# A graph layer's set-up reordered: the table of places turned, gather indices and raw rows' statistics moved

## The chip, the cores and the metric

The kernel runs on one core of a Trainium2 chip. The metric is the device time of one execution in microseconds (us), as the median over several executions; less is better. Below, PE is the matrix engine, PEld its weight loads, DVE the vector engine, ACT the scalar engine, POOL the GpSimd engine and SP the queue that issues most DMA transfers.

## What is computed

`x` holds 12,500 nodes with 128 features; 200,000 edges go from `src` to `dst` and are sorted by `dst`. The reference, cut down:

```python
h = jnp.maximum(_layernorm(x), 0.0)
Qv, Ku = h @ W_Q.T, h @ W_K.T
score = einsum('md,md->m', Qv[dst], Ku[src]) / sqrt(128) * exp(-edge_weight)
# of each dst node's edges keep the 16 of highest score; softmax over those
alpha = w / denom[dst]
agg = segment_sum(alpha[:, None] * (h[src] @ W_msg.T), dst)
out = x + relu(h @ W_self.T + agg)
```

## The kernel before

**Work units.** The edges are cut into 112 groups (`G`) of 14 chunks (`GC`) of 128 edges. For each chunk one indirect DMA, issued by POOL (`gather`, line 176), fetches 128 rows of 512 bytes into one of eight rotating tiles `hs`. A group takes 14 of them, so there are 1563 gathers in all (56 from `x`, 1507 from `h_tab`; the last group is short). POOL does hardly anything else.

**Raw groups.** Groups 0 to 3 (`RAW = 4`) are gathered from `x` itself, before the normalized table exists, and are normalized after the gather. All later groups are gathered from `h_tab`, a table of `relu(layernorm(x))` that the set-up writes to DRAM. Gathers from `h_tab` are let go two at a time by `let_go` (line 183): DVE copies two columns of indices into a small tile `ix`, and POOL waits for that copy. A gather of group g + 8 also waits until the last reader of group g's `hs` tile is done, which is the second half of `sums` (line 674) three passes after the group's own pass.

**Set-up (lines 278 to 421).** SP loads the source indices `src_r`, then `x` in six pieces, then weights, `dst_r` and `ew_r`, in that order. DVE clears tables, casts the indices (line 335), takes the statistics of `x`'s first piece (line 336), and copies the indices, turned by PE, to `idx_all` (line 338), which lets POOL begin. `row_stats` is one `bn_stats` for each row block (line 200), six small DVE operations and a square root on ACT (line 212). `normed` is a reciprocal and a product on DVE (lines 217 and 218) and one Relu activation on ACT for each row block (line 220). After `x`'s last piece, DVE makes from `dst_r` the tables `rel` (line 381), `h0` (384) and its running count `h1` (scan, line 386). PE turns them and DVE (line 397) and ACT (lines 400 and 401) write them to `pd`, a bfloat16 table of 128 x 112 x 2 x 16. For one edge of a chunk `pd` holds its place in its node's list and its node's distance in the group. ACT then writes the decay factors (line 402).

**Passes.** The main loop runs passes i from -3 to 117. It is a software pipeline: pass i makes the one-hot tables of group i + 1 (`edges_turned`, `far_of`, `away`, `to_edges`, `places`), the scores of group i, sorts scores into slots of group i - 1, picks the best 16 of group i - 2, and forms the weighted sums of group i - 3. The schedule is by hand: each engine executes its instructions strictly in the order of the program text, so an instruction that waits holds up all behind it on its engine.

On ACT a pass goes: the turned places `pdT` (line 550), four `far` squares (536), first `aw` square (559), two more `aw`, `to_e` (541), `hT` (517), `opo` (563). The `far` and `aw` matrices share one PSUM bank (`"a"`) with each other and with `sums`, so PE and ACT alternate there. In passes -1 to 2, `raw_stats(i + 1)` stands at the start of the pass, ahead of `pdT` on ACT through its square root, and `raw_normed(i + 1)` stands between the first and second `aw`.

`later` (line 440) is a list of checks on `pd` and others, one DVE operation in each pass from pass 1 on. DVE's `best` (line 613) and `scores` (line 583) and the copies of `let_go` fill the rest.

Of the kernel before, what the change touches and what calls it, by code (L numbers as in the profile page):

```python
# [10 lines left out]
F32 = mybir.dt.float32  # L11
BF16 = mybir.dt.bfloat16
# [8 lines left out]
P = 128  # L21
# [35 lines left out]
def lead(j):  # L57
    return STEP * j - PRE
# [7 lines left out]
def upper(ap):  # L66

    return ap.bitcast(BF16).rearrange("p (n two) -> p n two", two=2)[:, :, 1]
# [8 lines left out]
def gnn_layer(  # L77
# [35 lines left out]
    assert G > TAIL  # L113
# [41 lines left out]
    pd = const.tile([P, G, 2, 16], BF16, name="pd")  # L155
    dlw = pd[:, :, 1, 0:NJ]
# [23 lines left out]
    def gather_at_once(g, table):  # L180
        gather(g, 0, own[g], lambda j: idx_all[:, GC * g + j:GC * g + j + 1], table)

    def let_go(g, k):

        j0, j1 = 2 * k, min(2 * k + 2, own[g])
        if j0 >= j1:
            return
        if k == 0:
            T[g]["ix"] = rows_pool.tile([P, GC], I32, name="ix", bufs=7)
        ix = T[g]["ix"]  # L190
        nc.vector.tensor_copy(ix[:, j0:j1], idx_all[:, GC * g + j0:GC * g + j1])  # L191
        gather(g, j0, j1, lambda j: ix[:, j:j + 1])

    def row_stats(pool, rows, n, name, between=lambda: None):

        st = pool.tile([rows.shape[0], n, 6], F32, bufs=1, name=f"st{name}")
        for t in range(n):
            if t == 3:
                between()
            nc.vector.bn_stats(st[:, t, :], rows[:, t, :])  # L200
# [10 lines left out]
        nc.vector.tensor_scalar(rs, rs, 1.0 / D, EPS, op0=OP.mult, op1=OP.add)  # L211
        nc.scalar.sqrt(rs, rs)
        return rs, sm

    def normed(rows, n, rs, sm):

        nc.vector.reciprocal(rs, rs)
        nc.vector.scalar_tensor_tensor(sm, sm, -0.5, rs, op0=OP.mult, op1=OP.mult)
        for t in range(n):
            nc.scalar.activation(rows[:, t, :], rows[:, t, :], AF.Relu, bias=sm[:, t:t + 1],  # L220
                                 scale=rs[:, t:t + 1])

# [17 lines left out]
    with tc.tile_pool(name="edges", bufs=1) as ep, ExitStack() as stage:  # L240
# [48 lines left out]
        make_identity(nc, ident)  # L289
        nc.gpsimd.iota(dst_r, pattern=[[1, RL + P]], base=1 << 21, channel_multiplier=0)  # L290
# [3 lines left out]
        for p0, p1 in sixteens(1, k):  # L294
# [4 lines left out]
        nc.gpsimd.iota(slots, pattern=[[1, KM]], base=0, channel_multiplier=0,  # L299
                       allow_small_or_imprecise_dtypes=True)  # L300
        nc.gpsimd.iota(nvec, pattern=[[0, 1]], base=0, channel_multiplier=1,
                       allow_small_or_imprecise_dtypes=True)

        jj, eq = (alz[0][0:32, NJ * KM * k:NJ * KM * (k + 1)].rearrange("p (j k) -> p j k", k=KM) for k in range(2))
        nc.gpsimd.iota(jj, pattern=[[1, NJ], [0, KM]], base=0, channel_multiplier=0,
                       allow_small_or_imprecise_dtypes=True)
# [9 lines left out]
        nc.vector.memset(pd, 1.0)  # L316
        nc.vector.memset(dec_all[:, RR * CPR:CW], 0.0)
        nc.vector.tensor_scalar(minus, nvec, -1.0, None, op0=OP.mult)
        for j in range(NJ):
            nc.vector.memset(w0[:, j:j + 1], float(lead(j)))  # L320
# [8 lines left out]
        nc.vector.memset(alz[0], 0.0)  # L329
        for k in range(2):  # L330
            nc.vector.memset(sl1[k][:, :, KM:], 1.0)


        src_f = src_r.bitcast(F32)[:, 0:RW]
        nc.vector.tensor_copy(src_f, src_r[:, 0:RW])
        stat = {0: row_stats(prep, xs[0][2], sizes[0], "x0")}
        by_chunk = lambda t: t[:, 0:RR * CPR].rearrange("e (p j) -> e j p", j=CPR)
        to_columns(src_f, 0, lambda at, p: nc.vector.tensor_copy(at(by_chunk(idx_all)), p))
        for g in range(min(RAW, G)):
            gather_at_once(g, x)  # L340

        def finish(i):
            t0, n, xg = xs[i]
            normed(xg, n, *stat[i])
# [37 lines left out]
        let_go(RAW, 2)  # L382
        nc.vector.memset(h0[:, 0:1], 0.0)
# [3 lines left out]
        let_go(RAW, 4)  # L387
        bb = rows_pool.tile([P, 2, G], F32, name="bb")
        nc.vector.tensor_copy(bb, pb[:, 0:2 * G].rearrange("p (a g) -> p a g", a=2))

        for j0 in range(0, NJ, 4):
            j1 = min(j0 + 4, NJ)
            pt = bank("q", 3)
            for j in range(j0, j1):
                nc.tensor.matmul(pt[:, (j - j0) * RR:(j - j0 + 1) * RR], lhsT=rel[:, j * P:(j + 1) * P],
                                 rhs=upper(ident[0:RR, 0:RR]), start=True, stop=True)
            nc.vector.tensor_tensor(dlw.rearrange("e g j -> e j g")[:, j0:j1, :],
                                    pt[:, 0:(j1 - j0) * RR].rearrange("e (j g) -> e j g", g=RR),
                                    bc(w0[:, j0:j1], RR), op=OP.subtract)
        to_columns(h1, HALO, lambda at, p: nc.scalar.copy(at(pd[:, :, 0, :].rearrange("e g j -> e j g")), p))  # L400
        nc.scalar.copy(pd[:, 0:G - 1, 0, GC:NJ], pd[:, 1:G, 0, 0:1])
# [30 lines left out]
    def all_checked():  # L432
# [15 lines left out]
        lambda: nc.vector.tensor_reduce(badc[:, 0:1], pd[:, :, 0, 0:NJ], axis=AX.XY, op=OP.max),  # L448
# [32 lines left out]
    with tc.tile_pool(name="win", bufs=2) as win:  # L481
# [23 lines left out]
        def raw_stats(g):  # L505
            T[g]["raw"] = row_stats(rows_pool, T[g]["hs"], own[g], "r")

        def raw_normed(g):
            normed(T[g]["hs"], own[g], *T[g]["raw"])


# [195 lines left out]
        def at(g, stage, *args):  # L707
            if 0 <= g < G:
                stage(g, *args)


        for i in range(-3, G + 6):
# [5 lines left out]
            if i + 1 < RAW:  # L718
                at(i + 1, raw_stats)

# [29 lines left out]
            if i + 1 < RAW:  # L750
                at(i + 1, raw_normed)
# [28 lines left out]
            at(i, scores_in_slots)  # L780
            more(6)
# [187 lines left out]
```

## Time and profile before

| what | value |
|---|---|
| median of 4 runs | 2058.99 us (2058.85 to 2059.57) |
| the profiled execution | 2056.74 us |
| its span, first to last instruction | 2054.9 us |
| what lies around the span | 1.84 us |
| busy in the span | PE 81%, POOL 74%, DVE 62%, ACT 51% |
| mean granted PE clock | 0.896 |
| first gather begins | 15.75 us |
| last gather begins | 2010.53 us |

The profile is of one execution. "Busy" counts time inside instructions; a gather counts 0.94 us and is followed by at least 0.30 us in which POOL issues it, so POOL can be full at 74%. A line of the timeline is: start in us, length in us, engine, line of the kernel, operation, output<-inputs, and in brackets how long the engine was idle before and what ended that. A line of the waits is: total us, number of times, longest.

### The profile page before, as it was taken

To read this page: it belongs to the slowest core of one execution; us is meant where nothing else is said; L and a number is where in the kernel's file an instruction comes from. 1 tells how busy PE (TensorE), PEld (TensorE's weight loads), DVE (VectorE), ACT (ScalarE), POOL (GpSimd) and SP (SyncE) were. 2 spreads that over 40 slices of the span, in tenths; PEclk is the share of its full clock that TensorE was granted. 3 is DMA by queue.
4 is the path that set the end of the run, shared out by engine and by line. 5 is a ranking of instruction groups with operands and counts; after the bars stand their busy time and mean duration, and the time that the engine had idled before them with its cause. 6 is when DMAs were issued, how large, how long until landed. Compare 5 with 4: busy or idle time off the path is not lost. (4 is left out here: it accounts for less than half of the span.)

```text
span 2054.9 us, 42100 instructions
## 1 busy us (share of the span) xinstructions
PE 1658.2 (81%) x13800; PEld 1327.1 (65%) x13801; DVE 1272.3 (62%) x6998; ACT 1044.5 (51%) x2198; POOL 1511.0 (74%) x1580
## 2 busy tenths in 40 slices
PE   0367899999888898888888888889888888888895
PEld 0246777777666676666667676667676666666674
DVE  7547767676666656565656665666566556666653
ACT  6756555555444454444544444555455444445440
POOL 5775777777777777777777777777777777777772
PEclk9958999999998989898988988998889898989987
DMA  9511222222222222222222222222222222222210
GB/s 228 168 57 46 74 68 66 68 65 69 65 64 63 65 65 65 65 64 65 65 66 64 65 62 63 65 65 65 65 64 65 65 65 65 65 61 66 65 57 18
DMA packets 101472, 143.46 MB, mean 70 GB/s; under 512 B 31063, under 2 KB 74327, under 8 KB 100480
## 3 DMA queue, kind: packets, MB, share of 16 engines
q0 software_dynamic: 50144, 102.74, 17.6%
q1 hardware_dynamic: 51102, 37.99, 6.7%
q8 instruction: 108, 1.77, 0.4%
q14 instruction: 118, 0.97, 0.2%
HBM read 126.79 MB, written 14.40 MB: 69 GB/s over the span
## 5 line engine op out<-in xcount | busy, mean ns | idle before, releaser
L176 POOL DMA_INDIRECT hs<-h_tab,ix x1507 | 1442.4, 957 | 475.1 <-issue 278.9
L583 DVE SCALAR_TENSOR_TENSOR prod<-hs,dec_all,q 128x128 f32<-128x128 f32 x1674 | 499.4, 345 | 184.2 <-DMA hs<-h_tab,ix 144.9
L574 PEld LDWEIGHTS q<-q,to_e 128*128 128x128 f32 x3348 | 482.0, 217 | 73.6 <-issue 59.7
L574 PE MATMUL q<-q,to_e 128*128 128x128 f32 x3348 | 525.8, 306 | 0.0
L536 ACT ACTIVATE far<-a,minus 128x512 bf16<-128x512 f32 (+1 forms) x447 | 295.2, 660 | 374.5 <-PE a L534 365.7
L674 PE MATMUL a<-hs,alz 128*128 128x128 f32 x3348 | 450.2, 290 | 11.1 <-ACT aw L559 0.4
L674 PEld LDWEIGHTS a<-hs,alz 128*128 128x128 f32 x3348 | 420.0, 203 | 22.0 <-ACT aw L559 18.5
L613 DVE TENSOR_SCALAR ell<-slots,e 128x40 f32<-128x40 f32 x112 | 28.7, 256 | 472.6 <-PE e L599 469.1
L599 PEld LDWEIGHTS e<-opo,sl 128*41 128x41 f32 x3348 | 178.6, 134 | 101.3 <-issue 90.0
L534 PE MATMUL a<-rel,ident 112*128 112x512 bf16 (+1 forms) x447 | 192.2, 430 | 43.8 <-ACT far L536 26.9
L559 ACT ACTIVATE aw<-a 128x400 bf16<-128x400 f32 x336 | 168.6, 502 | 110.3 <-PE a L557 110.3
L599 PE MATMUL e<-opo,sl 128*41 128x40 f32 x3348 | 219.4, 224 | 0.0
L541 ACT ACTIVATE to_e<-far 128x1920 f32<-128x1920 bf16 x112 | 200.5, 1790 | 0.0
L557 PE MATMUL a<-minus_at,pdT 32*128 32x400 bf16 x336 | 119.7, 356 | 92.6 <-ACT aw L559 76.6
L682 PE MATMUL s<-ident,agn 128*128 128x128 f32 x112 | 40.2, 359 | 155.1 <-DVE o L694 150.5
L679 ACT ACTIVATE agn<-a,rden 128x128 f32<-128x128 f32 x112 | 41.2, 368 | 206.7 <-PE a L674 206.7
L583 DVE DVE_READ_ACCUMULATOR prod<-hs,dec_all,q 128x1 f32 x1674 | 140.7, 84 | 0.0
L563 ACT ACTIVATE opo<-aw 128x1200 f32<-128x1200 bf16 x112 | 136.1, 1215 | 0.0
L191 DVE COPY ix<-idx_all 128x2 int32<-128x2 int32 x754 | 128.7, 184 | 0.0
L682 PEld LDWEIGHTS s<-ident,agn 128*128 128x128 f32 x112 | 16.5, 148 | 168.4 <-DVE o L694 160.6
L642 PEld LDWEIGHTS <-to_e 128*128 128x128 bf16 x1674 | 52.1, 99 | 98.6 <-DVE prod L583 85.4
L550 ACT CAST pdT<-a 32x128 bf16<-32x128 f32 x112 | 28.5, 254 | 162.1 <-PE a L547 162.1
(172 smaller groups left out, 1737.3 us busy)
## 6 DMA issues: line engine op xcount, KB each, us to landing
hs<-h_tab,ix POOLq DMA_INDIRECT x1507
h_r<-h_tab SPq DMA_DIRECT2D x112, 64.0 KB
x_t<-in_x_dram SPq DMA_DIRECT2D x108, 64.0 KB
out_dram<-o SPq DMA_DIRECT2D x108, 64.0 KB
xg<-in_x_dram SPq DMA_DIRECT2D x2, 1400.0 KB
h_tab<-xg SPq DMA_DIRECT2D x2, 1400.0 KB
xg<-in_x_dram SPq DMA_DIRECT2D x1, 1120.0 KB
h_tab<-xg SPq DMA_DIRECT2D x1, 1120.0 KB
```

Source lines behind the costliest of these rows:

```text
L176: nc.gpsimd.indirect_dma_start(out=T[g]["hs"][:, j, :], out_offset=None, in_=table[0:N, :], in_offset=bass.IndirectOffsetOnAxis(ap=index(j ...
L191: nc.vector.tensor_copy(ix[:, j0:j1], idx_all[:, GC * g + j0:GC * g + j1])
L534: nc.tensor.matmul(pr[:, 0:n1 - n0], lhsT=upper(ident[0:RR, g:g + 1]).to_broadcast([RR, P]), rhs=rel[:, n0:n1], start=True, stop=True)
L536: nc.scalar.activation(T[g]["far"][:, n0:n1], pr[:, 0:n1 - n0], AF.Square, bias=minus)
L541: nc.scalar.activation(T[g]["to_e"][:, 0:n], T[g]["far"][:, 0:n], AF.Relu, bias=1.0, scale=-1.0)
L557: nc.tensor.matmul(pr[:, 0:400], lhsT=T[g]["pdT"], rhs=minus_at.rearrange("k w j s -> k (w j s)")[:, n0:n1], start=True, stop=True)
L559: nc.scalar.activation(T[g]["aw"][:, n0:n1], pr[:, 0:400], AF.Square)
L563: nc.scalar.activation(T[g]["opo"].rearrange("e w j s -> e (w j s)"), T[g]["aw"], AF.Relu, bias=1.0, scale=-1.0)
L574: nc.tensor.matmul(pq[:, (j - j0) * P:(j - j0 + 1) * P], lhsT=T[g]["to_e"][:, j * P:(j + 1) * P], rhs=T[g]["q"], start=True, stop=True)
L583: nc.vector.scalar_tensor_tensor(prod, rows_of(g, j), dec_all[:, c:c + 1], T[g]["pq", b][:, (j % 4) * P:(j % 4 + 1) * P], op0=OP.mult, op1 ...
L599: nc.tensor.matmul(et[0:KM + 1, STEP * j:STEP * j + WN], lhsT=sl1[g % 2][:, j, :], rhs=T[g]["ow"][:, j, :], start=False, stop=(j == n - 1))
L674: nc.tensor.matmul(T[g]["pa"][:, 0:P], lhsT=alz[g % 2][:, WW * j + PRE:WW * j + PRE + P], rhs=rows_of(g, j), start=(j == 0), stop=(j == n ...
```

## The change

- **The places' table is turned.** `pd` becomes `[128, 32, 112]`: the group number is now the innermost index. Lines 397, 400 and 401 write runs of 112 neighbours, where they wrote single elements 64 bytes apart. Instead of one memset over `pd`, two rows of it and two elements are set. The weight load of `edges_turned` (line 547) and the checks on `dlw` (lines 430 and 444) read elements 224 bytes apart, where they read neighbours.
- **Indices ahead of `x`'s statistics.** The cast of the indices is split (first 4 chunks of columns, then the rest). The statistics of `x`'s first piece come behind the index copies and the raw gathers in program order. Three small POOL operations come before the long `dst_r` iota. The memsets of `w0`, `alz[0]` and `sl1` move from ahead of the cast to behind `x`'s statistics.
- **Raw groups.** The statistics of groups 0 and 1 come directly behind `x`'s statistics in the set-up; their norming comes behind `rel` and behind the scan. The statistics of groups 2 and 3 and the norming of the first row block of each come at the end of pass 0; the other 13 row blocks of group 2 are normed at the end of pass 1 and those of group 3 at the end of pass 2. The tiles of the statistics have two names (`r0`, `r1`).
- `q` has two buffers where it had three.

```diff
-    pd = const.tile([P, G, 2, 16], BF16, name="pd")
-    dlw = pd[:, :, 1, 0:NJ]
+    pd = const.tile([P, 32, G], BF16, name="pd")
+    dlw = pd[:, 16:16 + NJ, :].rearrange("e j g -> e g j")
...
-    def normed(rows, n, rs, sm):
-        nc.vector.reciprocal(rs, rs)
-        nc.vector.scalar_tensor_tensor(sm, sm, -0.5, rs, op0=OP.mult, op1=OP.mult)
-        for t in range(n):
+    def normed(rows, n0, n1, rs, sm):
+        if n0 == 0:
+            nc.vector.reciprocal(rs, rs)
+            nc.vector.scalar_tensor_tensor(sm, sm, -0.5, rs, op0=OP.mult, op1=OP.mult)
+        for t in range(n0, n1):
             nc.scalar.activation(rows[:, t, :], rows[:, t, :], AF.Relu, bias=sm[:, t:t + 1],
                                  scale=rs[:, t:t + 1])
+    def raw_stats(g):
+        T[g]["raw"] = row_stats(rows_pool, T[g]["hs"], own[g], f"r{g % 2}")
+    def raw_normed(g):
+        normed(T[g]["hs"], 0, own[g], *T[g]["raw"])
+    def raw_begun(g):
+        normed(T[g]["hs"], 0, 1, *T[g]["raw"])
+    def raw_finished(g):
+        normed(T[g]["hs"], 1, own[g], *T[g]["raw"])
...
-        nc.vector.memset(pd, 1.0)
+        for k in (15, 31):
+            nc.vector.memset(pd[:, k, :], 1.0)
+        nc.vector.memset(pd[:, GC:NJ, G - 1:G], 0.0)
...
-        for j in range(NJ):
-            nc.vector.memset(w0[:, j:j + 1], float(lead(j)))
...
-        nc.vector.memset(alz[0], 0.0)
-        for k in range(2):
-            nc.vector.memset(sl1[k][:, :, KM:], 1.0)
-        nc.vector.tensor_copy(src_f, src_r[:, 0:RW])
-        stat = {0: row_stats(prep, xs[0][2], sizes[0], "x0")}
+        nc.vector.tensor_copy(src_f[:, 0:4 * P], src_r[:, 0:4 * P])
+        nc.vector.tensor_copy(src_f[:, 4 * P:], src_r[:, 4 * P:RW])
         to_columns(src_f, 0, lambda at, p: nc.vector.tensor_copy(at(by_chunk(idx_all)), p))
-        for g in range(min(RAW, G)):
+        for g in range(RAW):
             gather_at_once(g, x)
+        stat = {0: row_stats(prep, xs[0][2], sizes[0], "x0")}
...
+        for j in range(NJ):
+            nc.vector.memset(w0[:, j:j + 1], float(lead(j)))
+        nc.vector.memset(alz[0], 0.0)
+        for k in range(2):
+            nc.vector.memset(sl1[k][:, :, KM:], 1.0)
+        for g in range(2):
+            raw_stats(g)
...
         let_go(RAW, 2)
+        raw_normed(0)
...
         let_go(RAW, 4)
+        raw_normed(1)
...
-            nc.vector.tensor_tensor(dlw.rearrange("e g j -> e j g")[:, j0:j1, :],
+            nc.vector.tensor_tensor(pd[:, 16 + j0:16 + j1, :],
...
-        to_columns(h1, HALO, lambda at, p: nc.scalar.copy(at(pd[:, :, 0, :].rearrange("e g j -> e j g")), p))
-        nc.scalar.copy(pd[:, 0:G - 1, 0, GC:NJ], pd[:, 1:G, 0, 0:1])
+        to_columns(h1, HALO, lambda at, p: nc.scalar.copy(at(pd), p))
+        nc.scalar.copy(pd[:, GC:NJ, 0:G - 1], pd[:, 0:1, 1:G])
...
-            T[g]["q"] = win.tile([P, D], F32, name="q", bufs=3)
+            T[g]["q"] = win.tile([P, D], F32, name="q", bufs=2)
...
-            nc.tensor.matmul(pr[0:32, 0:P], lhsT=pd[:, g, :, :].rearrange("e w j -> e (w j)"), rhs=upper(ident),
+            nc.tensor.matmul(pr[0:32, 0:P], lhsT=pd[:, :, g], rhs=upper(ident),
...
-            if i + 1 < RAW:
-                at(i + 1, raw_stats)
...
             at(i + 1, away, 0)
-            if i + 1 < RAW:
-                at(i + 1, raw_normed)
...
             at(i, scores_in_slots)
+            if i == 0:
+                raw_stats(2)
+                raw_stats(3)
+                raw_begun(2)
+                raw_begun(3)
+            if i in (1, 2):
+                raw_finished(i + 1)
             more(6)
```

More of the change, by code (lines that the diff above doesn't have):

```diff
@@ L112, in gnn_layer @@
     G = -(-CH // GC)
-    assert G > TAIL
+    assert G > TAIL + 2
     EG = GC * P
@@ L289, in gnn_layer @@
         make_identity(nc, ident)
+        nc.gpsimd.iota(slots, pattern=[[1, KM]], base=0, channel_multiplier=0,
+                       allow_small_or_imprecise_dtypes=True)
+        nc.gpsimd.iota(nvec, pattern=[[0, 1]], base=0, channel_multiplier=1,
+                       allow_small_or_imprecise_dtypes=True)
+        jj, eq = (alz[0][0:32, NJ * KM * k:NJ * KM * (k + 1)].rearrange("p (j k) -> p j k", k=KM) for k in range(2))
+        nc.gpsimd.iota(jj, pattern=[[1, NJ], [0, KM]], base=0, channel_multiplier=0,
+                       allow_small_or_imprecise_dtypes=True)
         nc.gpsimd.iota(dst_r, pattern=[[1, RL + P]], base=1 << 21, channel_multiplier=0)
@@ L298, in gnn_layer @@
         load_rows(ew_r, ew)
[L299 to L306, printed above, removed]
         nc.gpsimd.memset(alz[1], 0.0)
@@ L328, in gnn_layer @@
                                            op0=OP.mult, op1=OP.subtract)
-        nc.vector.memset(alz[0], 0.0)
-        for k in range(2):
-            nc.vector.memset(sl1[k][:, :, KM:], 1.0)
         src_f = src_r.bitcast(F32)[:, 0:RW]
-        nc.vector.tensor_copy(src_f, src_r[:, 0:RW])
-        stat = {0: row_stats(prep, xs[0][2], sizes[0], "x0")}
+        nc.vector.tensor_copy(src_f[:, 0:4 * P], src_r[:, 0:4 * P])
+        nc.vector.tensor_copy(src_f[:, 4 * P:], src_r[:, 4 * P:RW])
         by_chunk = lambda t: t[:, 0:RR * CPR].rearrange("e (p j) -> e j p", j=CPR)
         to_columns(src_f, 0, lambda at, p: nc.vector.tensor_copy(at(by_chunk(idx_all)), p))
-        for g in range(min(RAW, G)):
+        for g in range(RAW):
             gather_at_once(g, x)
+        stat = {0: row_stats(prep, xs[0][2], sizes[0], "x0")}
         def finish(i):
             t0, n, xg = xs[i]
-            normed(xg, n, *stat[i])
+            normed(xg, 0, n, *stat[i])
             for a, b in cuts:
@@ L447, in gnn_layer @@
                                                op1=OP.mult, accum_out=badc[:, 2:3]),
-        lambda: nc.vector.tensor_reduce(badc[:, 0:1], pd[:, :, 0, 0:NJ], axis=AX.XY, op=OP.max),
+        lambda: nc.vector.tensor_reduce(badc[:, 0:1], pd[:, 0:NJ, :], axis=AX.XY, op=OP.max),
         lambda: nc.vector.tensor_scalar(badc[:, 0:1], badc[:, 0:1], float(KM), None, op0=OP.is_ge),
@@ L502, in load_nodes @@
                 nc.sync.dma_start(T[g]["x_t"], x_end[ds(start_of(g, 1, XT), P), :])
[L505 to L509, printed above, removed]
         def h_turned(g):
```

## Prediction

> **What bounds the kernel now.** The page's chain of work explains only the last 3 us, so I went by the groups, then POOL's waits, then the timelines of POOL, PE, ACT and DVE up to 185 us.
>
> ```profile
> L176 POOL DMA_INDIRECT hs<-h_tab,ix x1507 | 1442.4, 957 | 475.1 <-issue 278.9
> ```
>
> ```profile
> 164.32 0.94 POOL L176 DMA_INDIRECT hs<-h_tab,ix  x1 [0.30 <-issue]
> 179.57 0.94 POOL L176 DMA_INDIRECT hs<-h_tab,ix  x1 [14.31 <-ACT up L659]
> 182.64 1.44 POOL L176 DMA_INDIRECT hs<-h_tab,ix  x1 [2.12 <-issue]
> ```
>
> The first line: a gather is 0.96 us busy, and 0.3 us go between two. From 182.64 to the last gather's start at 2010.53, 1449 steps take 1827.9 us, 1.26 us each, and POOL's longest wait there is 0.3 us. So from 182.64 on the end hangs on POOL: whatever shifts that instant shifts the end by as much, and what DVE, ACT and PE do later is hidden. The 44 us from the last gather's start to the end are left as they are (only PE's clock, which moves there between 1.00 and 0.50, may fall otherwise: some 3 us either way, in the range).
>
> The other three lines are the 112th gather (the last of group 7), the 113th and the 114th. The 113th waits 14.31 us. It needs group 0's tile free and the `ix` copy of pass 3. The releaser named (ACT L659) had nothing to give; the PE timeline has the real one, and DVE's copy had ended at 178.7:
>
> ```profile
> 177.06 1.95 PE L674 MATMUL a<-hs,alz 128*128 128x128 f32 x16
> ```
>
> This ends at 179.01, POOL starts 0.56 later. **So the end is set by when pass 3 sums group 0**, and not by when POOL begins. An earlier first gather only lengthens the 14.31 us. The sum is therefore made along ACT, DVE and PE from the end of `x`'s statistics to pass 3, using these rows (ACT and DVE timelines):
>
> ```profile
> 71.45 7.06 ACT L400 CAST pd<-q 128x448 bf16<-128x448 f32 x4 [9.05 <-PE q L272]
> 108.95 5.48 ACT L220 ACTIVATE hs<-hs,smr,rsr 128x128 f32<-128x128 f32 x14
> 122.44 0.21 ACT L212 ACTIVATE rsr<-rsr 128x14 f32<-128x14 f32 x1 [3.60 <-DVE rsr L211]
> 145.67 0.21 ACT L212 ACTIVATE rsr<-rsr 128x14 f32<-128x14 f32 x1 [5.41 <-DVE rsr L211]
> ```
>
> ```profile
> 66.31 7.45 DVE L397 TENSOR_TENSOR pd<-q,w 128x448 bf16<-128x448 f32 x4
> 118.66 2.80 DVE L200 BATCH_NORM_STATS2 str<-hs 128x6 f32<-128x128 f32 x14
> ```
>
> The reader sees the slow table writes (1.86 and 1.77 us a step), the norming of a raw group (0.391 us a row block), and ACT held up by a raw group's statistics at the head of passes 1 and 2.
>
> **The change, step by step** (times on the profiled execution's axis; "+" is later than before).
>
> *1. POOL's start.* The first gather is at 15.75; ahead of it on DVE go the memsets of `pd` (3.04) and `alz[0]` (2.06), and the first piece's statistics (12.69 to 14.54). The first source indices have landed by 8.4 by the DMA records. From the cast on, 4.05 us less 1.85 of statistics leave 2.2 to 2.8: first gather near 11, 4.6 us earlier. Worth nothing, by the 14.31 us. It costs a little: some three more gathers (64 KB each) share the DMA engines with `x`'s loads, which move about 210 KB a us there. DVE waits for `x`'s fifth piece until 34.08, and ACT norms without a break from 35.25 on, so all of it comes +0.85 (0 if the gathers stay behind the loads).
>
> *2. DVE from 55.55 (reciprocal of `x`'s last piece).* Added: memset of `alz[0]` and small ones 2.1, statistics of two raw groups at 3.7 each (77.11 to 80.80 in the trace): +9.5. DVE is 99% busy from 60 to 80 us, so this is no cover but path. `dst_f`, `rel`, `h0`, scan follow, with two reciprocal pairs of 0.45: the scan ends at 66.05 + 0.85 + 9.5 + 0.45 = 76.9.
>
> *3. Table writes.* No row has contiguous bfloat16 writes from PSUM of this size. Nearest: 600 floats at L653 in 0.77, and the float writes at a 56-byte step at L402 and L338, 0.71 and 0.70 for 448. I take 0.58 for L397 (four steps 2.2, was 7.45), 0.62 for L400 (2.5, was 7.06), 0.25 for L401 (was 1.01); bounds: half of that, and no gain at all (the last rival). L397 is hidden now: ACT norms group 1 from 77.6, behind the scan, until 83.1, and L400 stands behind that in ACT's order; before, ACT was idle 9.05 us there. Norming of group 0 (71 to 76.5) falls into that idle time. Then 83.1 + 2.5 + 0.25 + table load 1.28 + decay factors 2.7 = 89.9, against 83.15. `pdT` of pass -1: 84.69 + 6.75 - 0.3 (the square root ahead of it goes) = 91.15, **+6.45**.
>
> *4. Pass -1.* Its norming goes: the second `aw` ran at 96.52, its matmul had ended near 92.3. -4.2: **+2.3**.
>
> *5. Pass 0.* Norming goes: the second `aw` (114.33) could run at 111.0: -3.3. But now two groups' statistics (7.4) stand behind `scores_in_slots` (its end 118.67 becomes 118.67 + 2.3 - 3.3 + 0.5, half a us because the full clock of 104.2 to 107.7 is unlikely to fall there again: 118.15), and both square roots stand on ACT ahead of pass 1's `pdT`. Statistics end at 125.6; roots, reciprocals and two row blocks 1.5: `pdT` at 127.1, was 122.56: **+4.55**.
>
> *6. Pass 1.* Norming in mid-pass goes (135.73 against 132.25): -3.5; `opo`, the last of the pass, ends at 140.27 + 4.55 - 3.5 = 141.3. The 13 row blocks are 5.1, and ACT has nothing else to wait for: `pdT` at 146.4, was 145.79: **+0.6**. So "late in a pass" fills the 5.41 us that ACT waited, not more.
>
> *7. Pass 2.* Norming goes from between 153.44 and 158.92; the exponentials could start with DVE's maxima at 154.6 plus 0.3, behind their table load: -5.1. Pass end 165.31 + 0.6 - 5.1 = 160.8, 13 row blocks 5.1: 165.9, was 166.46: **-0.5**.
>
> *8. Pass 3 and the clock.* Clock and busy time by stretch:
>
> ```profile
> 107.70:165.70 58.00, 37.12 (x186) 27.14 (x186) 27.11 (x150) 37.86 (x81) 43.90 (x45) 0.50 0.20 58
> 165.70:220.00 54.30, 46.14 (x426) 36.31 (x425) 41.30 (x203) 30.32 (x65) 29.77 (x30) 1.00 0.16 46
> ```
>
> (columns: length, PE, PEld, DVE, ACT, POOL busy with counts, granted clock, DMA share, GB/s). Passes 0 to 2 run at half clock; it rose at 165.7, after PE was busy without a gap from 161.23, and pass 3 had it whole. With the change PE is done with pass 2 some 4 us before the norming ends. At half clock, pass 2 needed 7.75 us from `pdT` to the first `aw` (145.79 to 153.54), pass 3 at full clock 5.62; eight L574 matmuls 2.08 against 1.16. So 0 if the clock stays, 3.0 if it is half until the sums begin, 7.5 if the sums (3.75 at full clock) and the six L574 between them (0.83) run at half too. Pass 2, with an idle PE ahead of it, is the nearest row: I take **+3.0**.
>
> The Trainium skill (TensorE: Matmul & The Clock Gate, "What's actually happening") says that the clock halves after at least one idle window of some 3.4 us and returns after a busy one. This trace speaks for the first half (3.5 us of thin work at 104.2, then 0.50) and against the second: 0.50 held through PE's dense stretch at 124.9 to 132.6. By the page pass 3 would lose at most 3.4 us of half clock, some 1.7.
>
> *9. What else is costed at nothing.* The turned table is now read with a 224-byte step: `edges_turned`'s weight load (0.093 for 32 columns). If a strided read cost what the strided write costs (1.86/448, 4.2 ns), that is +0.13 a pass, 0.5 up to pass 3, hidden by POOL later. L430 could take 7 instead of 1.90, in DVE's idle time before 152.60; L444 the same, after 182.64, under POOL's lead of four groups. The skill (SBUF — State Buffer, "Door 1") has a penalty for each access that changes its 16-byte line, which speaks against this change's reads; but L402's and L338's 56-byte steps show none, so here it is 2-byte elements that pay. By the page the reads would add the 0.5 above. `q` with two buffers waits for nothing: its tile's last reader is in the pass before. SP's queue and the `ix` copies keep their order.
>
> *Sum:* -0.5 + 3.0 = **+2.5 us**. The profiled execution, 2056.74, would be 2059.2; the median of the runs lies 2.25 above it, so 2058.99 + 2.5 = **2061.5**. About 0.2% (4.1 us) is what a measurement of this kernel can tell from no change.
>
> **Rivals.**
> - *Forecast, about the same*: the waits of ACT move from the heads of passes 1 and 2 to the end of pass 0 and the set-up. 2061.5, between 2055 and 2063. Chance 0.44.
> - *Faster: the clock rises earlier.* Passes 1 and 2 have no more norming in their middle, so PE's work is denser. If full clock holds from pass 1 on, each of passes 1 and 2 saves the 3.0 of step 8 and pass 3 loses none: -0.5 - 6.0 = -6.5, **2052.5**. For it: the windows at half clock have 64% busy PE. Against: PE still stands for 9 us behind the statistics of pass 0 and 4 to 5 us behind each late norming. Chance 0.19.
> - *Slower: half clock through pass 3's sums.* PE idles at the end of pass 2, and ACT and PE alternate in one bank; from the point where the clock is still half when L674 begins, +7.5 - 0.5 = +7.0: **2066.0**. Chance 0.30.
> - *Slower: contiguous writes gain nothing.* ACT and the reads are then late by L400's and L401's 5.3 more: +7.8, **2066.8**. It takes 2-byte writes that are slow at any step. Chance 0.07.
>
> **Range and chances.** 2052.0 to 2068.0 takes in all four with the unknowns of steps 1, 3 and 9. Faster 0.19, within 0.2% 0.44, slower 0.37; the forecast's own range is 2055 to 2063.
>
> **What the profile after would show.** First gather near 11; POOL's one long wait grown to 17 to 21 us and the next gather at 182 or so, instead of 179.57; L397 and L400 near 0.6 each; ACT idle (7 us) behind DVE's statistics before pass 1; PE's clock at 0.50 when pass 3 begins. The prediction is wrong if POOL's long wait is gone (then the start did count), if the statistics of groups 2 and 3 find DVE idle, or if POOL has waits over 0.4 us after 190.

## The result, and the profile after

The changed kernel takes 2055.37 us (median of 32 runs, 2050.97 to 2059.49) against 2058.44 us before (median of 52 runs, 2054.02 to 2062.03), measured on one chip. The ratio is 0.9986, 95% interval 0.9981 to 0.9991. So it is **faster by 0.14%, 3 us**, where the forecast was 2.5 us slower. Measured a second time (below) the ratio is 0.9983, 0.9974 to 0.9992. The size lies within the 0.2% of "about the same", the sign is the other one, and the interval leaves out 1.

The profiled execution took 2052.71 us (before 2056.74), its span is 2051.0 us. POOL's timeline shows the first gather, and the 112th, 113th and 114th:

```profile
10.63 1.11 POOL L176 DMA_INDIRECT hs<-in_x_dram,idx_all  x1 [4.27 <-DVE idx_all L349]
...
165.03 0.95 POOL L176 DMA_INDIRECT hs<-h_tab,ix  x1 [0.30 <-issue]
176.23 0.94 POOL L176 DMA_INDIRECT hs<-h_tab,ix  x1 [10.26 <-DVE prod L598]
179.30 1.44 POOL L176 DMA_INDIRECT hs<-h_tab,ix  x1 [2.12 <-issue]
```

PE's timeline shows again what the 113th waits for, the second half of group 0's sums (`sums`, L674 before and L689 now), which ends at 175.59 (before: 179.01):

```profile
173.64 1.95 PE L689 MATMUL a<-hs,alz 128*128 128x128 f32 x16
```

The wait is still there, and the 113th gather starts 3.34 us earlier than before (179.57). The copy of the indices is the other thing that this gather needs. In the twelve traces of this document in which POOL waits over 1 us here, the gather starts 0.54 to 0.64 us behind the end of the sums and 0.22 to 0.88 us behind that copy: the steady distance is the one to the sums.

From the 113th gather to the last one's start it is 1831.6 us, before 1831.0. **Most of what this execution gained was there at the 113th gather**: of the 3.9 us by which the span is shorter, 3.3 are gained up to there, 0.6 are lost up to the last gather, and 1.2 are gained behind it. These two later stretches also differ among the 14 traces of this document (1827.7 to 1832.6 us and 43.1 to 48.3 us), so a single execution does not settle a difference of 3 us. The first gather starts 5.1 us earlier (forecast: 4.6), but the 112th ends at 165.98, 0.7 us *later* than before; POOL's head start was used up on the way.

ACT's timeline, the set-up and the end of pass 0 (L221 is L220 before, L422 and L423 are L400 and L401):

```profile
67.02 0.22 ACT L212 ACTIVATE rsr<-rsr 128x14 f32<-128x14 f32 x1 [3.54 <-DVE row L384]
...
71.06 5.50 ACT L221 ACTIVATE hs<-hs,smr,rsr 128x128 f32<-128x128 f32 x14 [3.34 <-DVE smr L219]
77.54 5.50 ACT L221 ACTIVATE hs<-hs,smr,rsr 128x128 f32<-128x128 f32 x14 [0.98 <-DVE smr L219]
82.94 1.61 ACT L422 CAST pd<-q 128x448 bf16<-128x448 f32 x4
84.44 0.30 ACT L423 COPY pd<-pd 128x111 bf16<-128x111 bf16 x1
...
120.37 0.21 ACT L212 ACTIVATE rsr<-rsr 128x14 f32<-128x14 f32 x1 [2.34 <-DVE rsr L211]
124.01 0.21 ACT L212 ACTIVATE rsr<-rsr 128x14 f32<-128x14 f32 x1 [3.43 <-DVE rsr L211]
```

DVE's timeline, L419 being L397 before:

```profile
77.72 2.09 DVE L419 TENSOR_TENSOR pd<-q,w 128x448 bf16<-128x448 f32 x4
...
116.60 2.80 DVE L200 BATCH_NORM_STATS2 str<-hs 128x6 f32<-128x128 f32 x14
...
120.25 2.80 DVE L200 BATCH_NORM_STATS2 str<-hs 128x6 f32<-128x128 f32 x14
```

The table writes are cheap now (L422 1.61 us, before 7.06; L419 2.09, before 7.45). The raw groups' statistics keep ACT waiting twice in the set-up and twice at the end of pass 0.

Last, the stretches of 113th-gather time, cut at each `pdT` (passes -1 to 2, then pass 3 up to the end of the sums). Columns: length, busy time with counts of PE, PEld, DVE, ACT, POOL, then the granted clock, DMA share, GB/s. First passes 1 and 2 of the kernel before:

```profile
122.56:145.79 23.23, 14.82 (x73) 10.77 (x73) 11.54 (x60) 13.04 (x30) 17.75 (x19) 0.50 0.19 56
145.79:166.46 20.67, 14.90 (x88) 11.00 (x88) 9.69 (x53) 14.71 (x32) 14.90 (x16) 0.52 0.22 61
```

and passes 1, 2 and 3 of the changed kernel:

```profile
125.15:142.54 17.39, 11.64 (x73) 8.52 (x73) 8.62 (x36) 12.53 (x28) 13.51 (x13) 0.70 0.19 53
142.54:160.94 18.40, 12.18 (x88) 9.05 (x88) 11.44 (x53) 14.23 (x32) 14.44 (x14) 0.69 0.20 58
160.94:175.59 14.65, 13.47 (x107) 10.56 (x106) 7.62 (x48) 7.94 (x16) 3.82 (x5) 0.77 0.11 32
```

The clock column is the one to read. The forecast had 0.50 for all of passes 1 and 2; the trace has 0.70 and 0.69, which is 6.8 us at full clock in each.

### The profile page after: what moved, and what is told of

Its sections match the earlier page's. It is cut to its first block, busy times and chain, and to the rows that moved or that the text cites. A ratio compares the mean times of both kernels' runs of the same rounds, so it can differ in the third digit from the quotient of the medians.

```text
span 2051.0 us, 42115 instructions
## 1 busy us (share of the span) xinstructions
PE 1648.1 (80%) x13800; PEld 1321.4 (64%) x13801; DVE 1268.4 (62%) x7001; ACT 1040.3 (51%) x2198; POOL 1514.5 (74%) x1580
## 5 line engine op out<-in xcount | busy, mean ns | idle before, releaser
L589 PE MATMUL q<-q,to_e 128*128 128x128 f32 x3348 | 520.0, 303 | 0.0
L689 PE MATMUL a<-hs,alz 128*128 128x128 f32 x3348 | 447.3, 289 | 11.1 <-DVE alz L679 0.3
L689 PEld LDWEIGHTS a<-hs,alz 128*128 128x128 f32 x3348 | 417.0, 202 | 22.0 <-ACT aw L574 20.3
```

The lines of the kernel that those rows point to most:

```text
L589: nc.tensor.matmul(pq[:, (j - j0) * P:(j - j0 + 1) * P], lhsT=T[g]["to_e"][:, j * P:(j + 1) * P], rhs=T[g]["q"], start=True, stop=True)
L689: nc.tensor.matmul(T[g]["pa"][:, 0:P], lhsT=alz[g % 2][:, WW * j + PRE:WW * j + PRE + P], rhs=rows_of(g, j), start=(j == 0), stop=(j == n ...
```

## The experiments

Theory 1 is the prediction's: the end moves as much as the end of group 0's sums, and work on ACT, DVE and PE ahead of it sets that. Theory 2: the end moves with POOL's first gather. Theory 3: the passes got shorter only because the clock happened to fall well in that execution. Twelve kernels were run, three of them repeats. "Wait" is POOL's wait ahead of the 113th gather; all times are us from the start of the profiled execution; the ratio is to the kernel before, in runs on the same chip.

| kernel | ratio (95%) | first gather | 112th ends | wait | 113th starts | `pdT` of pass -1 | lengths of passes -1, 0, 1, 2, 3 |
|---|---|---|---|---|---|---|---|
| before | 1 | 15.75 | 165.26 | 14.31 | 179.57 | 84.69 | 18.0, 19.8, 23.2, 20.7, 14.2 |
| before_again | one run | 15.76 | 165.73 | 12.70 | 178.43 | 84.42 | 18.0, 19.3, 22.8, 20.8, 14.2 |
| after | 0.9986 (0.9981 to 0.9991) | 10.63 | 165.98 | 10.26 | 176.23 | 90.13 | 13.4, 21.6, 17.4, 18.4, 16.4 |
| after_again | 0.9983 (0.9974 to 0.9992) | 10.24 | 166.45 | 12.38 | 178.83 | 89.86 | 13.4, 21.4, 17.3, 18.2, 19.9 |
| table_only | 0.9978 (0.9968 to 0.9987) | 15.55 | 168.37 | 7.01 | 175.38 | 76.28 | 18.1, 20.3, 24.5, 21.2, 16.3 |
| index_only | 1.0019 (1.0010 to 1.0029) | 11.59 | 162.36 | 22.98 | 185.34 | 88.38 | 18.1, 20.8, 23.1, 20.4, 15.6 |
| raw_only | 1.0005 (0.9995 to 1.0016) | 15.75 | 169.34 | 13.75 | 183.08 | 93.83 | 13.4, 21.5, 17.4, 18.3, 19.9 |
| old_table | 1.0022 (1.0010 to 1.0033) | 11.60 | 165.15 | 18.77 | 183.92 | 94.89 | 13.4, 21.4, 17.3, 18.2, 19.8 |
| table_raw | 0.9966 (0.9955 to 0.9977) | 15.55 | 170.38 | 3.25 | 173.62 | 87.69 | 13.4, 22.2, 17.4, 18.4, 15.7 |
| hidden | 0.9909 (0.9894 to 0.9923) | 10.22 | 163.76 | 1.35 | 165.11 | 77.24 | 14.5, 19.4, 17.2, 18.2, 19.8 |
| hidden_again | 0.9920 (0.9906 to 0.9933) | 10.26 | 164.82 | 0.30 | 165.13 | 77.16 | 14.5, 19.4, 17.4, 18.4, 15.5 |
| hidden_late | 0.9929 (0.9916 to 0.9942) | 14.15 | 166.14 | 0.30 | 166.45 | 76.30 | 14.5, 19.4, 19.1, 18.2, 19.9 |
| hidden_reads | 0.9908 (0.9892 to 0.9923) | 10.70 | 163.37 | 2.68 | 166.05 | 77.94 | 14.5, 19.4, 17.3, 18.2, 19.9 |
| filler | 0.9974 (0.9964 to 0.9983) | 10.54 | 169.35 | 8.87 | 178.22 | 91.11 | 13.4, 22.2, 20.6, 16.7, 15.4 |

### The parts alone

**table_only** is the kernel before with the table turned and nothing else:

```diff
-    pd = const.tile([P, G, 2, 16], BF16, name="pd")
-    dlw = pd[:, :, 1, 0:NJ]
+    pd = const.tile([P, 32, G], BF16, name="pd")
+    dlw = pd[:, 16:16 + NJ, :].rearrange("e j g -> e g j")
...
-            nc.vector.tensor_tensor(dlw.rearrange("e g j -> e j g")[:, j0:j1, :],
+            nc.vector.tensor_tensor(pd[:, 16 + j0:16 + j1, :],
```

> Before with nothing but the turned table. Theory 1 (the end moves with the instant at which pass 3 sums group 0, so with the work on ACT and DVE ahead of it): the writes of lines 397, 400 and 401 cost what they cost in the changed kernel (2.1, 1.6 and 0.3 us instead of 7.4, 7.1 and 1.0), ACT stands idle there in the kernel before, so pass -1 begins some 6.7 us earlier, the 113th gather near 173 instead of 179.6, and the time falls by 6 to 7 us: more than the whole change gave. Theory 2 (the end moves with POOL's first gather): first gather stays at 15.75, no difference.

Measured: 2053.51 us, ratio 0.9978. The first `pdT` comes 8.4 us earlier, the 113th gather 4.2 us earlier. One part alone does at least as much as the whole change. It is still less than the 6 to 7 us expected: the set-up gained more than the 6.7 us, but pass 1 took back 1.3 us and pass 3 2.0 up to the 113th gather. In pass 3 the clock fell to half again for 3.4 us; what lengthened pass 1 is open.

**index_only** is the kernel before with the indices moved, the constants' memsets too:

```diff
+        nc.vector.tensor_copy(src_f[:, 0:4 * P], src_r[:, 0:4 * P])
+        nc.vector.tensor_copy(src_f[:, 4 * P:], src_r[:, 4 * P:RW])
...
+        stat = {0: row_stats(prep, xs[0][2], sizes[0], "x0")}
...
+        nc.vector.memset(alz[0], 0.0)
```

> Before with nothing but the indices ahead of x's statistics (and with the memsets that the change puts behind them). Theory 1: first gather near 10.6, but POOL only waits longer at the 113th; the memsets now stand on DVE's path and x's pieces land some 0.9 later, so the 113th gather comes about 3 us later and the time is 2 to 3 us more. Theory 2: the time falls by 3 to 5 us.

Measured: 2062.43 us, ratio 1.0019. POOL starts 4.2 us earlier and then waits longer, on its timeline:

```profile
161.41 0.95 POOL L176 DMA_INDIRECT hs<-h_tab,ix  x1 [0.30 <-issue]
185.34 0.94 POOL L176 DMA_INDIRECT hs<-h_tab,ix  x1 [22.98 <-DVE prod L585]
```

**Theory 2 falls**: 4.2 us of an earlier start became a longer wait, and the kernel is slower. The price is in DVE's timeline. The reciprocal of `x`'s last piece starts at 56.47 (before 55.55; of these 0.92 us the forecast put 0.85 on `x`'s loads beside the earlier gathers), and then 2.7 us of memsets stand on the path, which before stood ahead of the cast. Together the first `pdT` is 3.7 us later. The 113th gather is 5.8 us later, where about 3 were expected: the rest came in passes 0 and 3 (1.0 and 1.5 us), in which the clock was full for 3.4 and 4.0 us less than before.

**raw_only** is the kernel before with the raw groups' statistics and norming moved and `q` in two buffers, the table and the indices as before:

```diff
+        for g in range(2):
+            raw_stats(g)
...
-            if i + 1 < RAW:
-                at(i + 1, raw_stats)
...
+            if i == 0:
+                raw_stats(2)
+                raw_stats(3)
```

> Before with nothing but the raw groups' moves. Theory 1: the statistics of groups 0 and 1 and the norming of group 1 make pass -1 begin some 8.5 us later, and passes -1 to 3 are some 8.8 us shorter as they are in the changed kernel: within 1.5 us of before. Theory 3 (the passes got shorter only because PE's clock happened to fall well in the changed kernel): passes 1 and 2 at half clock as before, and the time 3 us more than before.

Measured: 2060.26 us, ratio 1.0005, no change. Passes -1, 1 and 2 are 4.7, 5.8 and 2.4 us shorter than before, the set-up is 9.1 us longer, pass 0 1.7, and pass 3, at half clock until 181.0, 5.6.

**old_table** is the changed kernel with the table as before:

```diff
-    pd = const.tile([P, 32, G], BF16, name="pd")
+    pd = const.tile([P, G, 2, 16], BF16, name="pd")
```

> The changed kernel with the table as it was before. Theory 1: ACT's writes cost 6.2 us more on the path, the 113th gather near 182, the time 2.5 to 3.5 us above before. Theory 2: as fast as the changed kernel, 3 us below before, since the first gather stays near 10.6.

Measured: 2064.7 us, ratio 1.0022, some 4.5 us above before where 2.5 to 3.5 were expected. Against the changed kernel the table is worth 0.0036 of the time, 7 us. The prediction's third rival (half clock through pass 3's sums) is to be seen here: pass 3 lasts 19.8 us, the 113th gather starts at 183.92.

**table_raw** leaves out the third part, the move of the indices:

```diff
-        stat = {0: row_stats(prep, xs[0][2], sizes[0], "x0")}
         by_chunk = lambda t: t[:, 0:RR * CPR].rearrange("e (p j) -> e j p", j=CPR)
         to_columns(src_f, 0, lambda at, p: nc.vector.tensor_copy(at(by_chunk(idx_all)), p))
```

(the line with the minus is in place again in this kernel, where the changed kernel has it behind the gathers).

> The kernel before with the turned table and with the raw groups' statistics and norming moved, but with x's first statistics again ahead of the index copies. Theory 1 (the end moves by as much as the sums of group 0 in pass 3, which release POOL's 113th gather): the move of the indices put nothing but time into the set-up, so the first turned edges come about 3 us before those of the changed kernel (87 against 90.1), the 113th gather at about 173 (176.2 in the changed kernel), and the time is 3 us below the changed kernel's, some 6 us below the kernel before (ratio 0.997). Theory 2 (the end moves with POOL's first gather): the first gather is back at about 15.7, so the time is some 3 us above the changed kernel's, as the kernel before's or worse.

Measured: 2051.77 us, ratio 0.9966; the 113th gather at 173.62, as theory 1 had it. So of the three parts **the turned table gains 4.5 us alone and 7.4 beside the two others, the raw groups' move little by itself, and the move of the indices costs about 4 us** (1.0019 alone; 0.9986 against 0.9966 with the two others).

### Was it the clock by chance?

**after_again** and **before_again** are the two kernels once more.

> The changed kernel itself, once more, for another execution's trace. Theory 1 with the clock as an effect of the passes' denser work: the granted clock is full for 6.8 us in pass 1 and in pass 2 again, and passes 1 and 2 last 17.2 to 17.8 and 18.0 to 18.6 us again. Theory 3 (the clock happened to fall well in that execution): at least one of the two passes is at half clock throughout and 1.5 to 2.5 us longer (19 to 20 and 20 to 21 us). Pass 3 is 16 to 16.5 us or, where the clock rises at its end, 19.5 to 20. The ratio to the kernel before is again 0.998 to 0.9995.

> The kernel before itself, once more, for another execution's trace. If the clock is an effect of the work in the passes: half clock through passes 1 and 2 again (23.2 and 20.7 us). If it is the phase of that execution: a stretch of 6.8 us at full clock in one of them, and that pass 1.5 to 2.5 us shorter.

Passes 1, 2 and 3 (to the end of the sums) of after_again, cut in the same way:

```profile
124.72:142.00 17.28, 11.66 (x73) 8.65 (x73) 8.38 (x37) 12.54 (x28) 13.62 (x13) 0.70 0.17 49
142.00:160.17 18.17, 11.99 (x88) 9.05 (x88) 11.43 (x53) 14.21 (x32) 14.21 (x14) 0.69 0.21 59
160.17:178.29 18.12, 17.64 (x107) 14.10 (x106) 9.48 (x54) 8.04 (x16) 4.76 (x6) 0.54 0.11 30
```

Passes 1 and 2 are the same, clock and all, so theory 3 falls for them. Over all kernels with the raw groups' work moved and no products added, the clock is full for 6.8 us in 17 of 18 of these passes. Pass 3 differs between two executions of one kernel: 14.65 us at 0.77, 18.12 at 0.54. That is 3.5 us in this pass and 2.6 us in the 113th gather's start, nearly as large as the change's whole effect. before_again shows 0.65 in pass 1 and is only 0.48 us shorter there, and index_only's pass 2, also with 6.8 us of full clock, is 0.23 us shorter than before's: with the statistics in the pass, the clock hardly matters. The two expectations for before_again were both partly wrong, then: the clock did rise by the phase of the execution, but the pass did not gain 1.5 us from it.

**filler** is the changed kernel with extra products in passes 1 to 3, called in three places of the pass:

```diff
+        def filled(i):
+            if i in (1, 2, 3):
+                for _ in range(4):
+                    nc.tensor.matmul(so[:, 3 * P:4 * P], lhsT=a_qk, rhs=wselfT, start=True, stop=True)
```

> The changed kernel with three times four extra TensorE products in each of passes 1, 2 and 3, whose results nobody reads: it leaves nothing out. Theory 1 with the granted clock as the cause of the passes' lengths: the clock is full for more of passes 1 to 3 than the 6.8 us in each that the changed kernel shows, pass 1 and 2 stay at 17 to 18.5 us or fall, pass 3 is not longer, and the 113th gather starts 0 to 4 us earlier (ratio to the changed kernel 0.998 to 1.000), with a smaller scatter. Rival: TensorE's own work is what the passes wait for, and 12 products of about 0.12 us at full clock and 0.24 us at half clock add 1.4 to 2.9 us to each pass: the 113th gather 4 to 8 us later (ratio to the changed kernel 1.002 to 1.004).

Its passes 1, 2 and 3 (to the end of the sums):

```profile
126.75:147.34 20.59, 19.44 (x97) 15.16 (x97) 8.48 (x36) 12.53 (x27) 16.17 (x15) 0.53 0.19 55
147.34:164.07 16.73, 12.39 (x113) 9.56 (x112) 11.43 (x53) 14.22 (x32) 12.77 (x14) 1.00 0.21 60
164.07:177.68 13.61, 12.70 (x123) 10.52 (x122) 8.99 (x52) 7.94 (x16) 4.06 (x5) 1.00 0.12 35
```

Both sides had a point. In pass 1 the rival is right: the clock stayed at half but for 1.2 us, and the pass is 3.2 us longer (1.5 us longer than hidden_late's pass 1 below, which is at half clock without the products). In passes 2 and 3 the clock is full, and they are 1.7 and 1.0 us shorter than after's, in spite of 12 and 8 more products (each shows as two records, so that pass 1 counts x97 for x73). The time, ratio 0.9974, is not to be told from the changed kernel's. The scatter was expected to shrink and did not: 11.0 us over 12 runs, for the changed kernel 8.5 over 32. What the clock is worth is shown, then, and how to hold it is not.

### The statistics where DVE is idle

**hidden** is the changed kernel with the raw groups' statistics and the memsets moved into gaps: those of group 0 ahead of `x`'s last norming, groups 1 and 2 at the end of pass -1, group 3 in pass 0. The norming of group 1 leaves the set-up too: one row block goes to the end of pass -1, the other 13 to the end of pass 0.

```diff
+                for j in range(NJ):
+                    nc.vector.memset(w0[:, j:j + 1], float(lead(j)))
+                nc.vector.memset(alz[0], 0.0)
+                for k in range(2):
+                    nc.vector.memset(sl1[k][:, :, KM:], 1.0)
+                raw_stats(0)
                 finish(i)
...
+            if i == -1:
+                raw_stats(1)
+                raw_stats(2)
+                raw_begun(1)
+                raw_begun(2)
...
-            if i in (1, 2):
+            if i in (0, 1, 2):
                 raw_finished(i + 1)
```

> The changed kernel with the raw groups' statistics put where VectorE idles: those of group 0 and the four sets of constants ahead of x's last norming (VectorE idles 6.6 us there in the changed kernel), groups 1 and 2 at the end of pass -1 (19.3 us idle), group 3 in pass 0. Theory 1: the 7.3 us of statistics leave the set-up and the 7.3 us at the end of pass 0 leave too, with ScalarE's waits of 2.3 and 3.4 us behind them. The first turned edges come at 77 to 82 instead of 90.1, group 0's sums end ahead of POOL's 112th gather, POOL's wait of 10.3 us falls to under 2 us and the 113th gather starts at 166 to 169: 7 to 10 us below the changed kernel, ratio to the kernel before 0.9935 to 0.995. Theory 2 (the end moves with POOL's first gather, which stays at 10.6): within 1.5 us of the changed kernel. A third way: the clock rises one window later since the passes begin earlier, and half of the gain is lost in pass 3 (ratio 0.996 to 0.997).

> The kernel 'hidden' itself, once more, beside the next one. Its time is 2040 to 2046 us, ratio to the kernel before 0.990 to 0.994; POOL's wait ahead of the 113th gather is under 2 us again; pass 1 is 17.2 us where the clock is full for 6.8 us in it and 19.1 where it is not.

Measured: 2040.08 us, and 2039.67 in the second run: ratios 0.9909 and 0.9920, more than expected and with hidden_reads (below) the fastest of all, **18.5 us below the kernel before** by the medians. In DVE's timeline group 0's statistics now stand where DVE waited 6.62 us, right up to the reciprocal of `x`'s last piece, which comes no later (54.99):

```profile
51.44 2.60 DVE L201 BATCH_NORM_STATS2 str<-hs 128x6 f32<-128x128 f32 x13
...
54.80 0.17 DVE L212 TENSOR_SCALAR rsr<-rsr 128x14 f32<-128x14 f32 x1
54.99 0.25 DVE L219 RECIPROCAL rsx<-rsx 125x15 f32<-125x15 f32 x1
```

POOL's long wait is gone. The 113th gather of hidden, and in the second line that of hidden_again:

```profile
165.11 1.82 POOL L176 DMA_INDIRECT hs<-h_tab,ix  x1 [1.35 <-ACT up L673]
```

```profile
165.13 0.94 POOL L176 DMA_INDIRECT hs<-h_tab,ix  x1 [0.30 <-ACT far L550]
```

In hidden_again 0.30 us is the usual step: POOL does not wait at all, the sums had ended at 160.65. The two traces gain 14.5 and 14.4 us at the 113th gather. hidden_again's last gather starts 17.7 us earlier than before's: 1.8 us more come in the step to the 114th gather (1.25 us, before 3.06), 1.4 in the steps behind it. hidden's trace is of the slowest of its four runs (2043.77 us), and loses 1.7 us behind the 113th.

Two moves are in this gain together and were not run apart: the statistics and memsets in the gaps, and the 5.5 us of group 1's norming that the changed kernel has on ACT just ahead of L422. The first `pdT` comes 12.9 us earlier than after's.

**hidden_late** puts the statistics of `x`'s first piece and `alz[0]`'s memset back ahead of the index copies, so that POOL starts 3.9 us later:

```diff
+        nc.vector.memset(alz[0], 0.0)
...
+        stat = {0: row_stats(prep, xs[0][2], sizes[0], "x0")}
         by_chunk = lambda t: t[:, 0:RR * CPR].rearrange("e (p j) -> e j p", j=CPR)
```

> The kernel 'hidden' with x's first statistics and one of the sets of constants put back ahead of the index copies, so that POOL's first gather starts at about 15.7 again and not 10.6. Both theories that name a wait say: where group 0's sums still end last (POOL's wait over 2 us in 'hidden'), this costs nothing or is a gain; where that wait is gone, POOL's own end sets the 113th gather, and the late start costs what is left of 5 us at the 112th gather's end, 3 to 5 us (ratio to the kernel before 0.9955 to 0.9975).

Measured: ratio 0.9929, whose interval overlaps hidden's. In the trace the 112th gather ends 1.3 to 2.4 us later than in the two traces of hidden, and the 113th starts at 166.45, 1.3 later. With the wait gone POOL's start does count, for about a third of what it is late by, and less than the 3 to 5 us expected; by the times alone this stays undecided.

The pair gives something else. From pass -1 on the two kernels have the same instructions, and pass 1 came once with 6.8 us of full clock and once without. hidden, then hidden_late:

```profile
111.16:128.32 17.16, 11.55 (x73) 8.64 (x73) 7.37 (x27) 12.52 (x27) 13.50 (x13) 0.70 0.17 50
```

```profile
110.21:129.33 19.12, 14.85 (x73) 10.80 (x73) 7.44 (x27) 12.53 (x28) 14.85 (x15) 0.50 0.19 55
```

DVE's and ACT's busy times are the same, PE's is 3.3 us longer and **the pass 1.96 us**.

**hidden_reads** is hidden with the check's working tiles turned too, so that it reads the table in its own order:

```diff
-    dlw = pd[:, 16:16 + NJ, :].rearrange("e j g -> e g j")
+    dlw = pd[:, 16:16 + NJ, :]
...
-            t.append(win.tile([P, G, NJ], F32, bufs=1, name="own_n" if t is own_n else "dl_n"))
-        nc.vector.tensor_tensor(dl[0], dlw, bm(w0, G), op=OP.add)
+            t.append(win.tile([P, NJ, G], F32, bufs=1, name="own_n" if t is own_n else "dl_n"))
+        nc.vector.tensor_tensor(dl[0], dlw, bc(w0, G), op=OP.add)
```

> The kernel 'hidden' with the check's working tiles turned as the table is, so that its reads of the table are contiguous again. If the step of 224 bytes is what made the check's first operation 3.25 us instead of 1.90 and its fourth 1.68 instead of 1.02, both fall back to 1.9 and about 1.0. In 'hidden' the first of them stands beside gathers that it lengthens (2.9 us of lengthening in the fourth pass's worth of gathers, 0.6 in the kernel before), so POOL's 112th gather ends 1 to 2 us earlier, but the 113th waits for group 0's sums as soon as POOL is ahead of them (1.35 us in 'hidden'): 0 to 1 us below 'hidden', ratio to it 0.9995 to 1.000.

DVE's first check in hidden, and then in hidden_reads:

```profile
122.60 3.22 DVE L451 TENSOR_TENSOR dl_n<-pd,w 128x1680 f32<-128x1680 bf16 x1
```

```profile
123.52 1.90 DVE L451 TENSOR_TENSOR dl_n<-pd,w 128x1680 f32<-128x1680 bf16 x1
```

The step did it (the fourth check falls from 1.68 to 1.03 as well). The time, ratio 0.9908, is hidden's.

## Why the prediction was wrong

The shift of each stretch against the kernel before, as forecast and in the two pairs of traces:

| step | forecast | after - before | after_again - before_again |
|---|---|---|---|
| 1 to 3, set-up | +6.45 | +5.44 | +5.44 |
| 4, pass -1 | -4.15 | -4.65 | -4.63 |
| 5, pass 0 | +2.25 | +1.80 | +2.11 |
| 6, pass 1 | -3.95 | -5.84 | -5.47 |
| 7, pass 2 | -1.1 | -2.27 | -2.60 |
| 8, pass 3 and the clock | +3.0 | +2.18 | +5.55 |
| sum, at the 113th gather | +2.5 | -3.34 | +0.40 |

**What bounds the kernel: right.** The end moved with group 0's sums, an earlier first gather was worth nothing (index_only, old_table), and POOL's start counted only in kernels where the wait was gone.

**The steps that failed are 6 and 7, by the sentence of step 8 that they rest on: "Passes 0 to 2 run at half clock".** That was a property of the kernel before, where the statistics and the norming stand in those passes, and it was carried over to passes that have lost them. The working itself was sound: at half clock the forecast's pass 1 is 23.23 - 3.95 = 19.28 us, and hidden_late, where pass 1 does run at half clock, has 19.12. With 6.8 us of full clock it is 17.2 to 17.4, the 1.96 us of the pair above. Steps 6 and 7 together miss by 3.1 us in the first pair of traces and by 3.0 in the second, more than any other step that missed both times the same way. Step 7's 1.2 to 1.5 us have the same look, the clock being 0.69, but no trace has such a pass 2 at half clock, so for pass 2 this is argued and not shown. The second rival had the right mechanism at 0.4 to 0.6 of its price, 1.9 and 1.2 a pass and not 3.0, since the clock was full for 6.8 us of a pass only. In filler, where it was full for all of pass 2, that pass took 16.73 us, 2.8 below the forecast's 20.67 - 1.1 = 19.57 at half clock.

**Step 3 was mis-sized by 1.0 us.** The four L400 steps were put at 2.5 us and took 1.61 (0.51 to 0.53 each, and 0.35 at the end); the rest of the chain came as worked out, L422 beginning at 82.94 where 83.1 was expected. "Contiguous writes gain nothing" fell.

**Step 5** added 0.5 us for a stretch of full clock that was thought unlikely to fall there again. It did fall there (at 106.2 in after, at 105.1 in after_again). The two ACT waits at the end of pass 0 came as worked out, 2.34 and 3.43 us behind 1.28 of table load.

**Step 8** was right in kind and its size is a lottery: +2.18 in one execution and +5.55 in the other, from the moment at which the clock rises in pass 3 (167.7 and 176.8). 3.0 lies in between. The second pair ends alike, 2055.66 us for after_again and 2055.62 for before_again. Two executions of the same program differ by more here than the two kernels do, so one pair of traces can't give the sign of this change; the many runs behind the ratio give it.

**POOL's wait** was to grow to 17 to 21 us and was 10.26 and 12.38. Part of that is the 113th gather, forecast at 182 and come at 176 to 179; the rest is POOL, whose head start of 5.1 us was 3.5 at the 28th gather, 1.3 at the 56th and gone at the 112th. Up to the 28th POOL waits 4.3 us in all beyond the usual 0.3 between two gathers, before 2.7, while `x` is loading. Later it waits again for earlier transfers (1.25 us at 63.5, 0.64 at 68.9), and gathers are lengthened beside long DVE operations. Of this the prediction said nothing, and it cost nothing, since POOL had 10 us to spare.

**Not seen by the prediction:** it called DVE "99% busy from 60 to 80 us" and put 9.5 us of statistics and memsets there as a given. The same trace has DVE idle for 6.62 us just ahead of it, and more in pass -1. hidden uses the two, and with group 1's norming moved as well gains six times what the change gains.

## What to carry to other kernels

Don't carry the clock of a pass over to that pass with less work in it: price it at both clocks, and keep both in the sum. Find the stretch where work is late (here up to the 113th gather), then look along the same engine for idle time just ahead of it that could hold the work; moving the raw groups' work from one loaded place to another gave nothing by itself here (raw_only, 1.0005), and moving it on into the gaps made the changed kernel some 15 us faster. And a change of several parts should be run part by part: one of the three cost 4 us and took back more than half of what another gained.

## What the runs showed of the hardware

**Reads at a 224-byte step of two-byte elements cost DVE** 3.25 us for 1680 elements against 1.90 (hidden_reads sets it back), and `edges_turned`'s weight load 0.135 us against 0.093. The prediction had put the first between 1.90 and 7 and the second at +0.13 at most.

**A gather beside a DVE operation that reads two tables is lengthened.** POOL's timeline in after, and under it the DVE operation beside it:

```profile
136.61 0.97 POOL L176 DMA_INDIRECT hs<-h_tab,ix  x1 [0.30 <-issue]
137.89 2.89 POOL L176 DMA_INDIRECT hs<-h_tab,ix  x1 [0.31 <-DMA hs<-h_tab,ix]
```

```profile
136.76 3.25 DVE L452 TENSOR_TENSOR dl_n<-pd,w 128x1680 f32<-128x1680 bf16 x1
```

The gather ends 0.8 us after the operation, at three times its usual length. In hidden_reads, where the operation is 1.90 us, the gather that outlasts it is 1.58 us. The Trainium skill (SBUF — State Buffer, "SBUF: two separate sides") says that a VectorE instruction with two SBUF inputs and a GpSimd instruction that reads SBUF exclude each other from a shared pair of ports, each for the whole of its length. These rows agree with it if a gather counts as such a reader (its indices lie in the tile `ix`); that this lock is the cause was not tried by itself.

**PE's work alone does not raise the clock at once.** In filler's pass 1 PE was busy 19.44 of 20.59 us, at 0.53. The granted stretches come in multiples of 3.4 us in every trace. In filler, over three such lengths, PE was busy all the time by the profile:

```profile
129.09:139.33 10.24, 10.24 (x58) 7.04 (x56) 2.49 (x18) 3.44 (x7) 7.55 (x9) 0.50 0.22 64
```

The clock stayed at 0.50 until 146.16. The Trainium skill (TensorE: Matmul & The Clock Gate, "What's actually happening") has the clock back after one busy window of some 3.4 us; this trace does not agree. What starts a full stretch is left open: of passes 1 and 2 without the raw groups' statistics, 17 of 18 had 6.8 us of full clock, and of those with them 2 of 8 (a third one had 3.4 us), but which part of the work decides was not found.
